# Moving a pair of reductions, a row of gathers and two small products in a two-layer graph attention kernel

## The chip, the cores and the metric

The kernel runs on one core of one Trainium2 chip. The metric is the time of one execution on the device in microseconds (us); lower is better. A core has TensorE (PE, matrix products; PEld is its loading of weights), VectorE (DVE), ScalarE (ACT), GpSimd (POOL) and SyncE (SP, which here only issues transfers). Each works through its own queue of instructions in order, and semaphores order the engines among each other. Transfers between memory and the core's SBUF run on 16 DMA engines.

## The reference, cut to what matters

The input `x` holds 16 graphs of 1024 nodes with 256 features; `adj` is a 1024 x 1024 adjacency matrix that all graphs share. Layer 0 is a small network with two attention steps, of which the first sees all pairs of nodes (no mask) and the second only the edges of `adj`. Layer 1 is one more masked attention.

```python
def _gat(inp, adj_mask, W, a):                 # layer 0
    h = inp @ W
    f1, f2 = h @ a[:F_, 0], h @ a[F_:, 0]
    e = leaky_relu(f1[:, :, None] + f2[:, None, :], 0.2)
    if adj_mask is not None: e = where(adj_mask > 0, e, NEG_INF)
    return elu(softmax(e, axis=2) @ h)

def _L0_gnn_ref(x, adj, ...):
    out = relu(x @ mlp1_w + mlp1_b);  residual = out
    out = elu(_gat(relu(out), None, W_fc, a_fc)) + residual      # dense attention
    out = relu(out @ mlp2_w + mlp2_b);  residual = out
    return relu(elu(_gat(relu(out), adj, W_hand, a_hand)) + residual)

def _L1_gnn_ref(inp, adj, W, a):               # slope 0.01, masked
    ...
    return relu(softmax(e, axis=-1) @ h)

x = x + _L0_gnn_ref(maximum(layernorm(x), 0), ...)
x = x + _L1_gnn_ref(maximum(layernorm(x), 0), ...)
```

## The kernel before, in words

Everything is float32. A graph is called `b` (0 to 15). Its nodes lie on the 128 partitions in 8 tiles `t`, which form two halves `h` of four tiles. The names on the profile's lines are tiles of the program: `hm` a projection, `att` a block of attention weights (128 x 256), `o` an accumulated product. An `a` at the end stands for the masked attention of layer 0 (`Gnn0`), a `b` for that of layer 1 (`Gnn1`).

The dense attention (`Dense`) computes no 1024 x 1024 matrix. Because the leaky ReLU of `f1 + f2` has two straight pieces, each node needs a sum over the nodes with small `f2` and one over those with large `f2`. So the rows of `h` are scattered to memory in the order of `f2` (`scatter`, L525) and read back sorted (`xs`). In each partition running sums are made over the 8 rows that it holds (`sum_before`, L597 and L599, in `tt`; `sum_behind`, L610 and L612, in `xs`), and `write_table` (L604) writes them to memory as the **fine** table. Two matrix products with triangles of ones (`carry`, L621) make the sums over the partitions before and behind; ACT copies them (L624), and SP writes them to memory as the **coarse** table (L626). For each node, `count` (L554) gives its row in both tables. `gather` (L637) is an indirect transfer that POOL issues: first the fine row of each of 128 nodes comes to the tile `got`, then the coarse row is added to it in flight. There are eight fine and eight coarse ones for a graph, four for each half, of 128 rows x 1026 numbers (525 KB) each; a coarse gather waits for the fine one of its tile. `share` (L649 to L652) makes the four tiles' denominators from `got`, and its first instruction waits for four coarse gathers. `mean` combines both sums of a tile (ACT's `part`, L659; DVE's `hp`, L661). `merge` transposes `hp` on PE (`hpT`, L708) and goes on with the ELU on DVE and ACT (L710 to L718); POOL adds the result to `resT` (L719). The second MLP (`mlp2`, L726) follows.

A masked attention projects its 8 tiles (`project`, L322, with ACT's copy to `hm`, L324). Then `extremes` (L329 and L330) takes the largest and smallest `f2` of each partition, and `vectors` brings the maxima to all partitions with a transpose on PE (`extps`, L238) and derives the factors `qwd`. For each quarter `q` of the rows DVE makes eight blocks of weights (L373) and PE multiplies them (L384). `Gnn0.finish` (L396 to L400) normalizes a tile, `combine` has POOL make two sums (L408 and L409), and `update` adds the outcome to `x` on DVE (L413). `Gnn1.finish` and `update` are L420 to L426, and `store` (L429) has SP write half of the output.

The second layer norm takes the statistics of each tile (L262 and L263), an inverse root for each half on POOL (`root`, L267 and L268), centers (`hn`, L272) and transposes on PE (`nt`, L282, with ACT's L286).

The order is written out by hand. `at(lo, hi, steps)` gives each step a due time on a ruler of the author's; the steps are sorted by it, and PE, DVE, ACT and SP take their instructions in that order. Added dependencies keep POOL's in the same order. A step puts all its instructions at one place in each queue that it uses. Graphs overlap: in the stretch of graph `b`, PE does the masked attention of layer 0 of `b` (`oa`), parts of that of layer 1 of `b - 1` (`ob`), the projection for layer 1 of `b` (`pb`), while the dense attention of `b + 1` goes through sums, gathers and merges, and the first MLP and projection of `b + 2` (L451 and L465) fill in. The stretches of `b` = 1 to 13 have one pattern. The first graph and the last two have due times of their own in part.

These are the due times that the change touches or meets, from the start `base` of the stretch of `b` on the ruler:

```python
gathers(dense[b + 1], h, base + 44.5 + 3.5 * h, base + 55 + 7 * h)    # b >= 1
# Gnn0.combine, tiles 4 to 7: 40.4, 41.0, 47.4, 48.0;  root: 43.0 and 56.5
# carry 0 and 1: 38.9, 45.9;  the products oa of quarter 1 end about 32, of quarter 2 about 39
# extremes of Gnn1: 78.5;  share of half 0: 78.0;  mean: 78.2 to 79.7
```

In memory, the buffer of `got` for the first half is that of `tt`, and that for the second half is that of `xs`; so the fifth fine gather waits for `carry(1)`, which reads `xs`. The first fine gather waits for the four writes of the fine table.

Of the kernel before, what the change touches and what calls it, by code (L numbers as in the profile page):

```python
# [31 lines left out]
def fast_path(ctx: ExitStack, tc: tile.TileContext, alarm, x, adj, w1, b1, w2, b2, w_fc, a_fc,  # L32
# [27 lines left out]
    NH = N // HALF  # L60
    TH = HALF // P
# [20 lines left out]
    def load_x(b, name):  # L82
        xt = big.tile([P, NT, F], F32, tag="x", name=f"{name}_{b}", bufs=3)
        src = x[b].rearrange("(t p) f -> p t f", p=P)
        for part in ((slice(0, TH), slice(TH, NT)) if name == "xn" and b == 0 else (slice(0, NT),)):
# [17 lines left out]
                            base=0, channel_multiplier=-1)  # L103
# [118 lines left out]
    def at(lo, hi, steps):  # L222
        for i, step in enumerate(steps):
            table.append((lo + (hi - lo) * i / len(steps), len(table), step))
# [74 lines left out]
    def tiles(h):  # L299
        return range(h * TH, (h + 1) * TH)  # L300
# [450 lines left out]
    norm1, norm2, dense, gnn0, gnn1 = {}, {}, {}, {}, {}  # L751
# [16 lines left out]
    def each(f, *ranges):  # L768
        out = [()]
        for r in ranges:  # L770
            out = [o + (i,) for o in out for i in r]
        return [partial(f, *o) for o in out]
# [14 lines left out]
    def first_mlp(t0, b):  # L787
        steps = mlp_steps(b)
        at(t0 + 0.7, t0 + 8, steps[:HC])
        lo = t0 + (39.3 if b == 2 else 78.1)  # L790
        at(lo, lo + 7, steps[HC:])

    def dense_rows(t0, b):

        for t in range(NT):
            at(t0 + BETWEEN[t], t0 + BETWEEN[t], [partial(dense[b].project, t, 1)])

    def dense_begin(t0, b):
        d = dense[b]
        at(t0 - 38.5, t0 - 38.5, [d.columns])  # L800
        at(t0 - 36.8, t0 - 36.8, [d.send, partial(d.row, True)])
        at(t0 - 31.5, t0 - 31.5, [d.highest])
        at(t0 - 28, t0 - 12, each(d.rank, range(NT)))
        at(t0 - 33, t0 - 30.5, [partial(d.project, t, 0) for t in range(2)])
        at(t0 - 21, t0 - 8, [partial(d.project, t, 0) for t in range(2, NT)])
        scatters(d, t0 - 18.5, t0 - 4.5)
        at(t0 - 6, t0 - 6, [d.query])
        at(t0 - 4, t0 - 4, [d.read_sorted])
# [5 lines left out]
    def dense_sums(t0, b):  # L814
        d = dense[b]
        at(t0 - 3, t0 - 3, [d.sums_begin])
        for t, lo in enumerate((27, 25, 18.5, 16.3, 14.1, 12, 9.8, 8.2)):
            at(t0 - lo, t0 - lo, [partial(d.sign, t)])
        for h in range(2):
            at(t0 + 6.5 + 4 * h, t0 + 6.5 + 4 * h, [partial(d.sums_weights, h)])  # L820
            at(t0 + 7.5 + 5 * h, t0 + 12.5 + 5 * h, each(d.sum_before, tiles(h)))
        at(t0 + 13, t0 + 13, [partial(d.write_table, 0, 0)])
        at(t0 + 18, t0 + 18, [partial(d.write_table, 0, 1)])
        at(t0 + 18, t0 + 32, each(d.sum_behind, range(NT - 1, -1, -1)))
        at(t0 + 25, t0 + 25, [partial(d.write_table, 1, 1)])
        at(t0 + 32, t0 + 32, [partial(d.write_table, 1, 0)])
        at(t0 + 33, t0 + 33, [d.count])
        at(t0 + 38.9, t0 + 38.9, [partial(d.carry, 0)])
        at(t0 + 45.9, t0 + 45.9, [partial(d.carry, 1)])

    def gathers(d, h, lo, hi):
        at(lo, lo + 4, each(d.gather, [h], [0], range(TH)))
        at(hi, hi + 7, each(d.gather, [h], [1], range(TH)))

    def dense_end(t0, b):
        d = dense[b]
        late = 10 * last(b)
        for h in range(NH):
            lo = t0 + late + 78 + 13.4 * h
            at(lo, lo, [partial(d.share, h)])  # L840
            lo = t0 + late + 78.2 + 14 * h
            at(lo, lo + 1.5, each(d.mean, [h], range(TH)))
            merges(t0 + late + 85 + 13.2 * h, d, h)
        second_mlp(t0, b)
# [17 lines left out]
    def masked_first(t0, b):  # L862
        m, n = gnn0[b], norm2[b]
        at(t0 + 1, t0 + 1, [m.vectors])
        lo = t0 + 11
        if b in AHEAD:
            at(t0 + 3.4, t0 + 3.4, [m.send])
            at(t0 + 6, t0 + 6, [partial(m.row, True)])
            lo += 7
        else:  # L870
            at(t0 + 4, t0 + 4, [m.row])
        at(t0 + 4.5, lo - 1, each(m.scale, range(NT)))
        weights(m, 0, lo - 5.5, lo - 1)
        at(t0 + 10, t0 + 10, [partial(load_again, b)])
        at(t0 + 4.5, t0 + 11, each(dense[b].natural, range(NT // 2)))
        at(lo, lo + 28, each(m.product, range(NQ), range(NT)))
        for q in range(1, NQ):
            weights(m, q, lo - 5.5 + 7 * q, lo + 1 + 7 * q)
        for t in range(NT):
            end = lo + 7.2 + 7 * (t // 2) + 0.6 * (t % 2)  # L880
            at(end, end, [partial(m.finish, t)])
            at(end + 1.2, end + 1.2, [lambda t=t: m.combine(t, dense[b].o_nat)])
            at(end + 5.2, end + 5.2, [lambda t=t: m.update(t, xs[b])])
            end += 6.2 if last(b) or b == 0 else 9
            at(end, end, [partial(n.stats, t)])
        at(lo + 25, lo + 25, [partial(n.root, 0)])
        lo += 35.5 if last(b) or b == 0 else 38.5
        at(lo, lo, [partial(n.root, 1)])

    def last(b, n=1):  # L890
        return b >= NB - n

    def second_norm(t0, b):
        n, m = norm2[b], gnn1[b]
        if last(b):
            n.turn_at(t0 + 46.5, 0)
            n.turn_at(t0 + 49, 1, 1.6)
            lo = t0 + 50
        elif b == 0:
            n.turn_at(t0 + 47, 0)  # L900
            n.turn_at(t0 + 50.5, 1, 1.6)
            lo = t0 + 47.2
        else:
            n.turn_at(t0 + 60.3, 0, 7)
            n.turn_at(t0 + 67.3, 1)
            lo = t0 + 71
        at(lo, lo + 7, each(m.project, range(NT)))
        at(lo + 7.5, lo + 7.5, [m.extremes])
        if last(b, 2):
            at(lo + 7.8, lo + 7.8, [m.vectors])  # L910
            at(lo + 8.2, lo + 8.2, [m.row])
            at(lo + 8.3, lo + 9.5, each(m.scale, range(NT)))
        else:
            at(lo + 11, lo + 11, [m.vectors])
            at(lo + 24, lo + 24, [m.send])
            at(lo + 40, lo + 52, each(m.scale, range(NT)))
            at(base_of(b + 1) - 4.5, base_of(b + 1) - 4.5, [partial(m.row, True)])

    def masked_second(parts, b):

        m = gnn1[b]
        for q, lo in enumerate(parts):
            at(lo, lo + 7, each(m.product, [q], range(NT)))
            weights(m, q, lo - 5.5, lo - 0.1)
            for u in range(2):
                t = 2 * q + u
                end = lo + 7.2 + 0.6 * u
                at(end, end, [partial(m.finish, t)])
                at(end + 1.5, end + 1.5, [lambda t=t: m.update(t, xs[b])])
            if q % 2:  # L930
                end = lo + 10
                at(end, end, [lambda h=q // 2: m.store(h, xs[b], b)])
# [7 lines left out]
    def base_of(b):  # L940
        return b * PERIOD - SHORT * (b > 0)

    START = -168.0
    n, d = norm1[0], dense[0]
# [34 lines left out]
    for t in range(TH):  # L979
        lo = START + 95 + 7.1 * t  # L980
# [31 lines left out]
    for b in range(NB):  # L1012
        base, after_base = base_of(b), base_of(b + 1)
        masked_first(base, b)
        second_norm(base, b)
        if last(b):
            parts = [base + 65 + 7 * q for q in range(NQ)]
        elif last(b, 2):
            parts = [base + 86, base + 94.5, base + 107.5, after_base + 39]
        else:  # L1020
            parts = [after_base + lo for lo in (11, 46, 53, 60)]
        masked_second(parts, b)
        if b + 1 < NB:
            if b:
                dense_sums(base, b + 1)
            for h in range(NH):
                if b:
                    gathers(dense[b + 1], h, base + 44.5 + 3.5 * h, base + 55 + 7 * h)
                else:
                    gathers(dense[1], h, base + 16 + 12 * h, base + 22 + 25 * h)  # L1030
            dense_end(after_base - PERIOD, b + 1)
        if b + 2 < NB:
            first_mlp(base, b + 2)
            dense_rows(after_base - PERIOD, b + 2)
            dense_begin(after_base, b + 2)
        if b + 3 < NB:
            lo = after_base - PERIOD + 86
            at(lo, lo, [partial(load_first, b + 3)])
            first_norm(after_base, b + 3)
# [465 lines left out]
```

## Time and profile before

| | |
|---|---|
| median of 3 runs | 2363.75 us (2357.47 to 2365.26) |
| the profiled execution | 2357.62 us, of which the span of the trace is 2355.9 us |
| mean granted TensorE clock | 0.99 |
| fine gather L637, 124 of them | 1.04 us of POOL each (mean), 5.6 us from issue to landing (median) |
| coarse gather L637, 124 of them | 1.60 us of POOL each (mean), 10.5 us from issue to landing (median) |
| one stretch of the repeating part | about 140 us |

A line of instructions in order of time gives start and duration in us, engine, source line, operation, output and inputs, and in brackets the idle time of the engine before it and what ended that. A line of waits reads: engine, tile and line that waited; what it waited for; us in total, number of times, longest. In a table of stretches each engine's busy time stands with the number of its instructions; the last three columns are the granted clock, the busy share of the DMA engines and their GB/s.

### The profile page before, as it was taken

How to read it: one execution, taken by the hardware profiler on the slowest of the kernel's cores; microseconds unless marked ns; L12 is line 12 of the kernel's file. 1: busy time of each engine (PE TensorE's matmuls, PEld its weight loads, DVE VectorE, ACT ScalarE, POOL GpSimd, SP SyncE). 2: the span in 40 equal slices, each digit the busy share in tenths (PEclk: the TensorE clock that was granted, in tenths of full speed). 3: DMA queues.
4: the chain of work that ended last, by engine and by line, in shares of the span. 5: the costliest groups of instructions: out<-in, count | busy, mean ns of one | idle time of the engine just before them, and what ended most of it. 6: DMA issues, size and time to landing. Idle time of an engine off the chain costs nothing. (4 is left out here: it accounts for less than half of the span.)

```text
span 2355.9 us, 30815 instructions
## 1 busy us (share of the span) xinstructions
PE 2264.0 (96%) x9955; PEld 1750.0 (74%) x9955; DVE 1610.9 (68%) x4499; ACT 1243.7 (53%) x2740; POOL 954.7 (41%) x1216
## 2 busy tenths in 40 slices
PE   8989999999999999999999999999999999999897
PEld 6666777777868778787877868777786877778676
DVE  6666685766858577685866767586685857668554
ACT  5355645647365564745546374554736556473442
POOL 1153435264433536434263533535344352634320
PEclk9999999999999999999999999999999999999898
DMA  4558356572655746366573645657264564636500
GB/s 175 166 161 206 74 167 172 168 189 96 191 127 175 184 149 183 96 193 151 170 188 128 178 112 173 163 170 201 96 196 118 171 179 152 184 95 193 122 1 29
DMA packets 150762, 355.81 MB, mean 151 GB/s; under 512 B 11112, under 2 KB 62648, under 8 KB 146496
## 3 DMA queue, kind: packets, MB, share of 16 engines
q1 hardware_dynamic: 103968, 189.58, 26.4%
q0 software_dynamic: 45952, 163.99, 26.3%
q8 instruction: 82, 1.34, 0.2%
q14 instruction: 88, 0.72, 0.1%
q10 hardware_dynamic: 672, 0.17, 0.0%
HBM read 227.40 MB, written 126.30 MB: 150 GB/s over the span
## 5 line engine op out<-in xcount | busy, mean ns | idle before, releaser
L384 PE MATMUL ob<-hmb,attb 128*128 128x257 f32 x2048 | 466.7, 386 | 13.6 <-DVE attb L373 13.5
L465 PE MATMUL h<-wfc_sb,resT 128*128 128x257 f32 x2048 | 465.5, 380 | 0.0
L384 PE MATMUL oa<-hma,atta 128*128 128x258 f32 x2048 | 454.4, 382 | 3.1 <-DVE atta L373 2.9
L384 PEld LDWEIGHTS ob<-hmb,attb 128*128 128x128 f32 x2048 | 388.3, 192 | 79.1 <-ACT rb L422 12.5
L384 PEld LDWEIGHTS oa<-hma,atta 128*128 128x128 f32 x2048 | 387.1, 190 | 65.1 <-DVE atta L373 9.6
L465 PEld LDWEIGHTS h<-wfc_sb,resT 128*128 128x128 f32 x2048 | 379.4, 190 | 53.5 <-issue 0.7
L719 POOL TENSOR_TENSOR resT<-resT,e 128x512 f32<-128x512 f32 x128 | 163.3, 1276 | 386.9 <-DVE e L718 343.4
L408 POOL TENSOR_TENSOR posa<-posa,onat 128x256 f32<-128x256 f32 x120 | 100.8, 840 | 468.2 <-ACT posa L400 467.6
L373 DVE SCALAR_TENSOR_TENSOR atta<-rowsa,qwda,edge 128x256 f32<-128x256 f32 x512 | 268.2, 554 | 24.0 <-PE oa L384 12.6
L373 DVE SCALAR_TENSOR_TENSOR attb<-rowsb,qwdb,edge 128x256 f32<-128x256 f32 x512 | 237.2, 505 | 9.9 <-PE ob L384 7.4
L451 PE MATMUL m<-hT,w_sb 128*128 128x512 f32 x512 | 236.2, 599 | 0.5 <-ACT posa L400 0.5
L726 PE MATMUL m<-resT,w_sb 128*128 128x512 f32 x512 | 231.5, 599 | 4.4 <-POOL resT L719 4.4
L422 ACT ACTIVATE rb<-ob,recb 128x256 f32<-128x256 f32 x128 | 59.1, 475 | 332.1 <-DVE recb L420 320.4
L637 POOL DMA_INDIRECT got<-coarse,k x124 | 198.1, 1598 | 39.0 <-issue 35.4
L399 ACT ACTIVATE ea<-oa,reca 128x256 f32<-128x256 f32 x128 | 60.8, 475 | 267.6 <-DVE reca L396 267.6
L710 DVE TENSOR_SCALAR e<-hpT 128x512 f32<-128x512 f32 x128 | 88.4, 690 | 141.3 <-PE hpT L708 108.8
L726 PEld LDWEIGHTS m<-resT,w_sb 128*128 128x128 f32 x512 | 94.1, 192 | 107.2 <-issue 91.3
L451 PEld LDWEIGHTS m<-hT,w_sb 128*128 128x128 f32 x512 | 93.0, 194 | 92.1 <-issue 89.7
L637 POOL DMA_INDIRECT got<-fine,k x124 | 128.9, 1040 | 55.4 <-DMA fine<-xs 23.9
L525 POOL DMA_INDIRECT sorted<-hnat,place x128 | 131.4, 1026 | 39.5 <-issue 20.3
L548 ACT ACTIVATE junk<-r,fs 128x1024 int8<-128x1024 f32 x124 | 142.4, 1149 | 5.7 <-POOL fs L469 4.7
L711 ACT ACTIVATE e<-e 128x512 f32<-128x512 f32 x128 | 80.7, 631 | 88.0 <-DVE e L710 87.9
(186 smaller groups left out, 3442.4 us busy)
## 6 DMA issues: line engine op xcount, KB each, us to landing
xs<-sorted SPq DMA_DIRECT2D x32, 1028.0 KB
fine<-tt SPq DMA_DIRECT2D x32, 1026.0 KB
fine<-xs SPq DMA_DIRECT2D x32, 1026.0 KB
x<-in_x_dram SPq DMA_DIRECT2D x16, 1024.0 KB
out_dram<-x SPq DMA_DIRECT2D x32, 512.0 KB
xn<-in_x_dram SPq DMA_DIRECT2D x15, 1024.0 KB
coarse<-carry SPq DMA_DIRECT2D x32, 256.5 KB
r<-row_r SPq DMA_DIRECT2D x14, 512.0 KB
```

The source lines that it names most:

```text
L373: nc.vector.scalar_tensor_tensor(a_t, self.rows[:, q * PAIR:(q + 1) * PAIR], self.qwd[:, 1, j:j + 1], edge[:, j, q * PAIR:(q + 1) * PAIR], ...
L384: nc.tensor.matmul(self.out[t][:, :F + self.ONES], lhsT=self.att[q, j][:, (t % 2) * P:(t % 2 + 1) * P], rhs=self.hm[:, j, 2:2 + F + self.O ...
L408: adder.tensor_add(pos, pos, o_nat[:, t, :])
L451: nc.tensor.matmul(ps, lhsT=w1_sb[:, kc, c * P:(c + 1) * P], rhs=hT[:, kc, h * HALF:(h + 1) * HALF], start=(kc == 0), stop=(kc == FC - 1))
L465: nc.tensor.matmul(ps[:, :F + 1], lhsT=self.resT[:, kc, t * P:(t + 1) * P], rhs=wfc_sb[:, kc, g, :], start=(kc == 0), stop=(kc == HC - 1))
L525: made = nc.gpsimd.indirect_dma_start(out=sorted_d[self.b % 2], out_offset=bass.IndirectOffsetOnAxis(ap=self.place[:, t:t + 1], axis=0), i ...
L548: nc.scalar.activation(junk, self.r2, AF.Sign, bias=self.fs[:, 0, t:t + 1], accum_out=self.signs[:, t:t + 1])
L637: nc.gpsimd.indirect_dma_start(out=got[u // n][:, u % n, :], out_offset=None, in_=(coarse_d if coarse else fine_d)[self.b % 2][:, :], in_o ...
L710: nc.vector.tensor_scalar_min(e, ps, 0.0)
L711: nc.scalar.activation(e, e, AF.Exp)
L719: nc.gpsimd.tensor_add(dst, dst, e)
L726: nc.tensor.matmul(ps, lhsT=w2_sb[:, kc, c * P:(c + 1) * P], rhs=self.resT[:, kc, h * HALF:(h + 1) * HALF], start=(kc == 0), stop=(kc == H ...
```

## The change

It does three things, all of them by other due times; no instruction is added or taken away.

1. `extremes` of the second layer's attention is due at `lo + 6.9` instead of `lo + 7.5`. In DVE's queue that puts L329 and L330 ahead of `share` of the first half; before, they stand behind `share` and the first `mean`. Nothing else changes its place on DVE.
2. From `b` = 1 on, `early_gathers` replaces `gathers`: the first four fine gathers are due at 41.5 and 42.5, the other four at 48.5 to 53, the coarse ones at 53.5 to 68. In POOL's queue, with S4 to S7 for the sums of a tile, F and C for fine and coarse gathers of the first (0) and second (1) half:

```
before, b = 1 to 3 and 8 to 14:  S4 S5 root0 F0 F0 F0 S6 F0 S7 F1 F1 F1 F1 C0 root1 C0 C0 C0 C1 C1 C1 C1
before, b = 4 to 7:              S4 S5 root0 F0 F0 F0 S6 F0 F1 S7 F1 F1 F1 C0 root1 C0 C0 C0 C1 C1 C1 C1
after:                           S4 S5 F0 F0 F0 F0 root0 S6 S7 F1 F1 F1 F1 C0 C0 root1 C0 C0 C1 C1 C1 C1
```

3. Both carries are due 7 earlier. On PE `carry(0)` moves from between the quarters 2 and 3 of `oa` to between 1 and 2, and `carry(1)` from behind quarter 3 to ahead of it. ACT's copies move with them, ahead of `finish` of tile 2 and of tile 4. On SP the write of the first carry moves ahead of the last write of the fine table.

```diff
-        at(t0 + 38.9, t0 + 38.9, [partial(d.carry, 0)])
-        at(t0 + 45.9, t0 + 45.9, [partial(d.carry, 1)])
+        at(t0 + 31.9, t0 + 31.9, [partial(d.carry, 0)])
+        at(t0 + 38.9, t0 + 38.9, [partial(d.carry, 1)])
...
+    def early_gathers(d, t0):
+
+        fine, coarse = [each(d.gather, range(NH), [s], range(TH)) for s in range(2)]
+        at(t0 + 41.5, t0 + 41.5, fine[:2])
+        at(t0 + 42.5, t0 + 42.5, fine[2:4])
+        at(t0 + 48.5, t0 + 53, fine[4:])
+        at(t0 + 53.5, t0 + 68, coarse)
...
-        at(lo + 7.5, lo + 7.5, [m.extremes])
+        at(lo + 6.9, lo + 6.9, [m.extremes])
...
-            for h in range(NH):
-                if b:
-                    gathers(dense[b + 1], h, base + 44.5 + 3.5 * h, base + 55 + 7 * h)
-                else:
+            if b:
+                early_gathers(dense[b + 1], base)
+            else:
+                for h in range(NH):
                     gathers(dense[1], h, base + 16 + 12 * h, base + 22 + 25 * h)
```

## The prediction

> **What bounds the kernel now.** I read the shares of busy time first, then the waits of TensorE, then one repeating stretch in order of time. TensorE (PE) is busy for 96% of the span, so at most some 92 us of idle time can be won; the table of PE's waits says where it lies.
>
> ```profile
> PE 2264.0 (96%) x9955; PEld 1750.0 (74%) x9955; DVE 1610.9 (68%) x4499; ACT 1243.7 (53%) x2740; POOL 954.7 (41%) x1216
> ...
> PE extpsb L238 <- DVE extb L330: 22.0, 13, 2.7
> PE nt L282 <- DVE hn L272: 15.4, 8, 9.7
> PE ob L384 <- DVE attb L373: 13.5, 20, 2.1
> PE hpT L708 <- DVE hp L661: 6.4, 7, 1.7
> ```
>
> The largest wait is for the two extremes of `extb` (L329, L330), which are tiny instructions. In order of time, 11 of the 13 stretches from `b` = 1 to 13 have it, 0.9 to 2.7 us each, 20.5 us together (two more of 0.76 us are in the last two elements and wait for another thing). Those of `hn` and `hpT` lie almost wholly at the beginning and the end. The order of time for `b` = 13 shows what the extremes stand behind (start, duration, engine; in brackets the idle time before and who ended it):
>
> ```profile
> 2048.09 1.55 POOL L637 DMA_INDIRECT got<-coarse,k  x1 [0.30 <-issue]
> ...
> 2058.43 0.16 DVE L649 TENSOR_TENSOR den<-got,qd 128x4 f32<-128x4 f32 x1 [9.60 <-DMA got<-coarse,k]
> ...
> 2059.99 0.75 DVE L661 SCALAR_TENSOR_TENSOR hp<-got,den,part 128x513 f32<-128x513 f32 x1 [0.79 <-ACT part L659]
> 2060.66 0.16 DVE L329 TENSOR_REDUCE extb<-hmb 128x1 f32<-128x8 f32 x1
> 2060.74 0.16 DVE L330 TENSOR_REDUCE extb<-hmb 128x1 f32<-128x8 f32 x1
> 2060.81 2.29 DVE L661 SCALAR_TENSOR_TENSOR hp<-got,den,part 128x513 f32<-128x513 f32 x3
> ```
>
> ```profile
> 2060.97 0.29 PE L238 MATMUL extpsb<-ident,extb 128*128 128x128 f32 x1 [1.84 <-DVE extb L330]
> 2061.10 1.88 PE L451 MATMUL m<-hT,w_sb 128*128 128x512 f32 x4
> 2062.82 0.67 PE L708 MATMUL hpT<-ident,hp 128*128 128x128 f32 x4
> ```
>
> The fourth coarse gather is issued at 2048.09 and lands after 10.2 us. The vector engine (DVE) sits idle for 9.60 us until then. In all 13 stretches PE starts L238 2.53 to 2.55 us after that landing, so PE is tied to the landing; and the next thing PE needs, `hpT`, comes only 1.85 us later and depends on the same landing.
>
> **What the skill says.** The Trainium skill, "DMA: Bandwidth & Descriptors", section "Issuing engines are not separate DMA queues", says that transfers of all issuing engines interleave on the same 16 DMA engines. The trace agrees, and shows where they are full (PE, PEld, DVE, ACT, POOL busy; then clock, DMA share, GB/s):
>
> ```profile
> 2035.00:2039.00 4.00, 3.93 (x20) 3.10 (x19) 3.70 (x12) 0.95 (x2) 3.24 (x4) 1.00 0.63 210
> 2039.00:2043.00 4.00, 4.00 (x24) 3.37 (x22) 3.66 (x13) 0.22 (x1) 3.31 (x5) 1.00 0.83 287
> 2043.00:2067.00 24.00, 22.16 (x95) 16.09 (x94) 9.71 (x30) 14.08 (x31) 12.15 (x9) 1.00 1.06 236
> ```
>
> "SBUF — State Buffer", section "Who interferes with whom", says that a DVE instruction with two SBUF inputs contends with a GpSimd instruction that reads SBUF. It agrees: L413 takes 0.41 us alone and 0.94 us beside GpSimd's (POOL's) sums. "PSUM — Partial Sum Buffer", section "Engine vs sequencer instructions", says that these engines' queues are strictly first in, first out; every start in these rows agrees.
>
> **Part 1, the extremes.** Nothing is added. They move ahead of `share` of the first half, to 2054.4, when the last `hmb` copy ends and DVE is idle: cost nothing, hidden in the 9.60 us. The 1.84 us wait goes. What is late next is `hpT`. PE would pass L238 at 2059.13 (2060.97 less 1.84), do 0.11 + 1.72 us of work to 2060.96, and then need four `hp` tiles. They end at 2063.10 now; with the two extremes (0.15 us together in issue) gone from between them, the second could end 0.15 us sooner, but the last two wait for ACT's `part` tiles, two buffers in turn at some 0.75 us each, which start when the first `hp` ends, at 2060.7, as now. I take 0.07 us (bounds 0 and 0.15). So 1.84 us of wait at L238 becomes some 1.8 us at L708: over 13 stretches the gain is 13 x 0.07 = 0.9 us, not 20.5.
>
> **Part 2, the gathers.** Only a sooner landing helps further. These rows are POOL's queue now:
>
> ```profile
> 2025.92 1.12 POOL L268 TENSOR_TENSOR rstd<-rstd,power 128x4 f32<-128x4 f32 x1
> 2027.24 1.12 POOL L637 DMA_INDIRECT got<-fine,k  x1 [0.20 <-issue]
> ...
> 2032.57 1.14 POOL L637 DMA_INDIRECT got<-fine,k  x1
> ...
> 2035.41 1.14 POOL L637 DMA_INDIRECT got<-fine,k  x1
> ...
> 2040.79 1.65 POOL L637 DMA_INDIRECT got<-coarse,k  x1 [0.30 <-issue]
> ```
>
> In the changed order all four fine gathers of the first half follow the sums of tile 5 in one row, then come `root(0)`, the sums of tiles 6 and 7, the other four, two coarse, `root(1)`, six coarse. They are not two and two between sums. From 2021.37 POOL has one gap, 0.90 us, before the sum of tile 4, and nothing is moved into it. So the first fine gathers start at 2025.6 instead of 2027.24, the fourth at 2029.5 instead of 2032.57; but the 5.2 us of four gathers, 1.6 us of `root(0)` and 2 x 1.5 us of sums end at 2035.3 in either order. The fifth gather stays at 2035.4, the first coarse at 2040.8, the fourth at 2048.1. Could the DMA engines still finish sooner? The fifth fine gather lands 5.4 us after its issue, as the very first does, so the earlier ones do not hold it up now. From 2043 the engines are full. What is unused between 2038.5 and 2043 is about 0.8 us (shares of 0.6 to 1.1 in half-microsecond slices), and only a sooner fifth gather could use it. The second coarse gather comes 1.3 us sooner, into full engines. I take 0 here (bound: 0.8 us gained).
>
> The loss: the sum of tile 6 ends at 2033.7 instead of 2032.4, so L413 and a weight (L373) that now run with POOL on gathers run beside the sum of tile 7. L413 goes from 0.42 to 0.94 us, L373 from 0.48 to 0.9; POOL's two adds go from 0.73 and 0.72 to 0.91 and 0.79. That puts the fifth gather about 0.2 us later, which the unused 0.8 us after it can take up: I take 0 at the landing (bound: 0.4 us lost a stretch). In four stretches (`b` = 4 to 7) two gathers stand ahead of the sum of tile 7 now, and PE loses 1.3 us there at L384 instead of 0.36; the change cures that, but PE waits for the landing afterwards all the same: nothing gained.
>
> `root(1)` moves behind the second coarse gather: it ends at 2045.9 instead of 2043.86. `hn` of the second half starts then instead of at 2044.96; queued behind it on DVE are two reciprocals, two updates and the second store of `out`, all about 1 us later. PE's transposes at 2045.96 wait for `hn`, a new wait of 0.7 us. It is hidden as long as PE has more than that before `hpT`, and it has about 1.8 us. In `b` = 14, with no such cover, I count 0.7 us. `root(0)` comes at 2032 and is needed at 2036.1: nothing.
>
> **Part 3, the carries.** Each is four passes, 0.87 us of PE, moved past 7 us of `oa` products; PE's total stays. The sums they read are done (`all_t` at 1997.7, the last `xs` at 2011.3; they would run at 2008 and 2015.9). ACT's copies go ahead of tiles 2 and 4, which wait for DVE until 2013.36 and 2020.45: nothing. SP's write of the first carry goes past the last fine write, ready about 2010 against 2011.3: nothing. PE reaches `oa`'s later products 0.87 us later, so seven waits for `atta` of 0.4 us may go; they too lie ahead of the landing.
>
> **The sum.** -0.9 + 0 + 0.7 = -0.2 us; with the bounds, -(0.15 + 0.8) x 13 = -12 and 0.4 x 13 + 0.7 = +6 us. On the profiled execution's own time, 2357.62 us (a span of 2355.9 and 1.7 around it), this is 2357.4. The median of the runs is 2363.75, 6 us above that execution, within the 8 us over which the runs spread; on it the sum gives 2363.5 us, no change. Within 0.3%, 7 us, is about what a measurement of this kernel cannot tell from nothing.
>
> **Rivals.** (a) The landing does move. If the early gathers and the second coarse one free the DMA engines, all the 0.8 us is won: 13 x 0.9 = 12 us, 2352 us; if the landing is 1.8 us sooner, the whole 20 us, 2344 us. For it: PE is tied to the landing in every stretch, so each 0.1 us there is 1.3 us. Against it: the fifth gather's unobstructed 5.4 us and a POOL queue without holes. The second half caps it: its `hp` are ready at 2076.8, just before PE's 2076.99. (b) Slower: POOL's sums of tiles 6 and 7, now back to back beside DVE's updates, hold back the fifth gather and with it both landings. At 0.4 us and with no part of it absorbed it is 5 us; it decides (over 7 us) from 0.55 us a stretch, and 0.8 us gives 13 x 0.8 = 10 us, 2374 us. For it: POOL is the link ahead of the DMA, with no slack. Against it: two DVE instructions only collide. (c) The change does not begin the gathers that matter sooner; that is my forecast.
>
> **How the numbers follow.** The forecast has 0.53, rival (a) 0.30, rival (b) 0.17. The range 2344 to 2373 takes in the whole of (a) and most of (b); the likeliest case alone is 2357 to 2370.
>
> **What would show it.** Right: PE's wait for `extb` falls from 22 us to some 2, and a wait of `hpT` for `hp` (L661) of 15 to 25 us stands in its place; the first coarse gather starts about 19.4 us after the sum of tile 4; `nt` waits some 0.7 us for `hn` in each stretch. Wrong: DVE's wait for the coarse landing ends more than 0.5 us sooner or later, counted from the sum of tile 4, or waits for `hp` stay under 8 us.

## The result, and the profile after

| | median, us | runs | lowest to highest |
|---|---|---|---|
| before | 2363.61 | 20 | 2354.8 to 2371.03 |
| after | 2356.84 | 20 | 2350.22 to 2361.55 |

The ratio is 0.9972, with a 95% interval of 0.9963 to 0.9980: 6.8 us, 0.28%, less. That lies within the 0.3% that the prediction called no change and inside its range, just below the 2357 to 2370 us of its likeliest case, but it is a gain all the same, and 6.6 us more than the sum of -0.2 us. The profiled execution took 2353.15 us with a span of 2351.4 us (before: 2357.62 and 2355.9).

The busy times of the page after:

```profile
PE 2271.9 (97%) x9955; PEld 1751.2 (74%) x9955; DVE 1620.2 (69%) x4499; ACT 1241.4 (53%) x2740; POOL 955.0 (41%) x1216
```

PE's busy time rose by 7.9 us though it does the same work. The groups of `nt` and `hpT` are 5.5 and 3.8 us longer, most likely because short waits inside a group count as busy, so a part of the waiting has only changed its name. The rest is in the table of PE's waits after (us in total, times, longest):

```profile
PE nt L282 <- DVE hn L272: 21.4, 23, 9.7
PE hpT L708 <- DVE hp L661: 11.8, 23, 1.7
PE ob L384 <- DVE attb L373: 11.6, 17, 2.1
...
PE extpsb L238 <- DVE extb L330: 1.5, 2, 0.8
```

The wait for `extb` went from 22.0 to 1.5 us, `hpT` from 6.4 to 11.8, and `nt` has 15 short waits more. The stretch of `b` = 13 after, in order of time, DVE first:

```profile
2050.96 0.17 DVE L329 TENSOR_REDUCE extb<-hmb 128x1 f32<-128x8 f32 x1 [5.48 <-ACT hmb L324]
...
2053.27 0.17 DVE L649 TENSOR_TENSOR den<-got,qd 128x4 f32<-128x4 f32 x1 [2.07 <-DMA got<-coarse,k]
```

The extremes stand alone ahead of the landing, and DVE waits twice, first for `hmb` and then for the landing. PE in the same stretch:

```profile
2042.11 1.43 PE L282 MATMUL nt<-ident,hn 128*128 128x128 f32 x8 [0.43 <-DVE hn L272]
...
2055.50 0.27 PE L238 MATMUL extpsb<-ident,extb 128*128 128x128 f32 x1
...
2057.33 0.85 PE L708 MATMUL hpT<-ident,hp 128*128 128x128 f32 x4
...
2059.76 0.60 PE L708 MATMUL hpT<-ident,hp 128*128 128x128 f32 x4
```

L238 has no wait left. The second group of `hpT` starts 6.48 to 6.50 us after the landing in all 13 stretches; before it was 6.63, in `b` = 13 here (the landing is at 2058.43):

```profile
2065.06 0.60 PE L708 MATMUL hpT<-ident,hp 128*128 128x128 f32 x4
```

So PE is still tied to the landing, one instruction further on. POOL, the sum of tile 4 before and then after:

```profile
2021.37 0.73 POOL L408 TENSOR_TENSOR posa<-posa,onat 128x256 f32<-128x256 f32 x1 [2.83 <-ACT posa L400]
```

```profile
2017.24 0.72 POOL L408 TENSOR_TENSOR posa<-posa,onat 128x256 f32<-128x256 f32 x1 [2.83 <-ACT posa L400]
...
2028.53 0.72 POOL L409 TENSOR_TENSOR ea<-ea,posa 128x256 f32<-128x256 f32 x1
2029.21 0.73 POOL L408 TENSOR_TENSOR posa<-posa,onat 128x256 f32<-128x256 f32 x1
2030.02 0.79 POOL L409 TENSOR_TENSOR ea<-ea,posa 128x256 f32<-128x256 f32 x1
2030.97 1.08 POOL L637 DMA_INDIRECT got<-fine,k  x1 [0.17 <-issue]
```

The fifth fine gather (2030.97) comes 13.7 us after the sum of tile 4; before it was 14.0. The first coarse one comes at 19.1 instead of 19.4.

Where the 4.5 us of span went: the first landing (`b` = 1) comes 1.9 us sooner, the twelve periods from there to the landing of `b` = 13 take 1673.52 instead of 1676.74 us, and the end takes 0.7 us more.

The landing is the number to follow. In every kernel below I took the start of L649 of the first half less the start of the sum of tile 4, and the same for the second half, each as a mean over the 13 stretches of the one profiled execution. Three kernels that leave the gathers where they were give 37.19, 37.37 and 37.39, so differences of 0.2 us are noise. The lost clock is the sum of 1 less the granted clock over a table of stretches of 1 us; what it means comes with the kernel one later.

| kernel | first half, us | second half, us | lost clock, 250 to 2150 us | ratio to before, 95% interval |
|---|---|---|---|---|
| before | 37.19 | 49.11 | 1.7 | 1 |
| after | 36.89 | 48.89 | 1.7 | 0.9972 (0.9963 to 0.9980) |
| extremes alone | 37.37 | 49.31 | 5.1 | 1.0001 (0.9990 to 1.0012) |
| gathers alone | 36.64 | 48.49 | 0 | 0.9961 (0.9946 to 0.9976) |
| carries alone | 37.39 | 49.34 | 3.4 | 1.0006 (0.9996 to 1.0017) |
| fine gathers early alone | 36.79 | 48.78 | 6.8 | 0.9978 (0.9966 to 0.9990) |
| second coarse gather ahead of root(1) alone | 37.01 | 48.95 | 1.7 | 0.9985 (0.9975 to 0.9995) |
| fourth coarse gather one later | 39.65 | 51.68 | 23.9 | 1.0194 (1.0167 to 1.0220) |
| first half first | 32.96 | 49.17 | 10.2 | 1.0006 (0.9992 to 1.0019) |
| in turn | 35.40 | 49.01 | 0 | 0.9962 (0.9948 to 0.9976) |
| after, stores late | 36.26 | 46.99 | 1.7 | 0.9953 (0.9938 to 0.9968) |
| before, stores late | 36.52 | 47.34 | 1.7 | 0.9940 (0.9916 to 0.9963) |
| in turn, stores late | 35.03 | 46.48 | 1.5 | 0.9904 (0.9877 to 0.9932) |
| the same without parts 1 and 3 | 34.51 | 45.86 | 1.7 | 0.9865 (0.9848 to 0.9881) |

The same starts divide each period in two: from the sum of tile 4 to the landing, and from the landing to the next sum of tile 4. The second part is 102.5 to 102.7 us on average in eleven of these kernels, before and after among them. So in these eleven, what an edit wins or loses in a stretch shows ahead of the landing. The three others are one later (103.8), in turn (103.7) and first half first (107.5), where PE pays behind the landing, as shown below.

### The profile page after: what moved, and what is told of

Same layout as the page of the kernel before. It is cut to its first block, busy times and chain, and to the rows that moved or that the text cites. A ratio compares the mean times of both kernels' runs of the same rounds, so it can differ in the third digit from the quotient of the medians.

```text
span 2351.4 us, 30828 instructions
## 1 busy us (share of the span) xinstructions
PE 2271.9 (97%) x9955; PEld 1751.2 (74%) x9955; DVE 1620.2 (69%) x4499; ACT 1241.4 (53%) x2740; POOL 955.0 (41%) x1216
## 5 line engine op out<-in xcount | busy, mean ns | idle before, releaser
L384 PE MATMUL ob<-hmb,attb 128*128 128x257 f32 x2048 | 467.7, 386 | 11.8 <-DVE attb L373 11.6
L465 PEld LDWEIGHTS h<-wfc_sb,resT 128*128 128x128 f32 x2048 | 379.5, 190 | 53.5 <-issue 0.7
L373 DVE SCALAR_TENSOR_TENSOR attb<-rowsb,qwdb,edge 128x256 f32<-128x256 f32 x512 | 243.6, 518 | 11.0 <-PE ob L384 8.4
```

Source lines behind the costliest of these rows:

```text
L373: nc.vector.scalar_tensor_tensor(a_t, self.rows[:, q * PAIR:(q + 1) * PAIR], self.qwd[:, 1, j:j + 1], edge[:, j, q * PAIR:(q + 1) * PAIR], ...
L384: nc.tensor.matmul(self.out[t][:, :F + self.ONES], lhsT=self.att[q, j][:, (t % 2) * P:(t % 2 + 1) * P], rhs=self.hm[:, j, 2:2 + F + self.O ...
L465: nc.tensor.matmul(ps[:, :F + 1], lhsT=self.resT[:, kc, t * P:(t + 1) * P], rhs=wfc_sb[:, kc, g, :], start=(kc == 0), stop=(kc == HC - 1))
```

## The experiments

### One part at a time

**Extremes alone.**

```diff
-        at(lo + 7.5, lo + 7.5, [m.extremes])
+        at(lo + 6.9, lo + 6.9, [m.extremes])
```

> The kernel before with part 1 alone: extremes due at lo + 6.9, gathers and carries as before. My theory (PE is tied to the landing of the fourth coarse gather, and the extremes only decide which wait stands there): the wait of extpsb for extb falls from 22.0 us to about 2, a wait of hpT for hp of some 1.5 us a stretch takes its place, the landing counted from the sum of tile 4 stays within 0.2 us of 37.2, and the time falls by 0.07 to 0.15 us a stretch, 1 to 2 us (ratio about 0.9995). Rival: the extremes are the whole change, and this kernel shows all of its 6.7 us (ratio 0.997).

Measured: 2361.60 us (14 runs), ratio 1.0001. PE's waits of this kernel:

```profile
PE hpT L708 <- DVE hp L661: 21.9, 43, 1.7
...
PE extpsb L238 <- DVE extb L330: 1.5, 2, 0.8
```

20.5 us of waiting left `extb` and 15.5 us came back at `hpT`. Together with 7 us that PE's group of `hpT` is longer "busy" (85.3 instead of 78.2) that makes up for all of it. The second `hpT` group starts at 6.49 us after the landing instead of 6.63, so the gain is 0.14 us a stretch, 1.8 us, too little to be seen in the time. The rival is out.

**Carries alone.**

```diff
-        at(t0 + 38.9, t0 + 38.9, [partial(d.carry, 0)])
-        at(t0 + 45.9, t0 + 45.9, [partial(d.carry, 1)])
+        at(t0 + 31.9, t0 + 31.9, [partial(d.carry, 0)])
+        at(t0 + 38.9, t0 + 38.9, [partial(d.carry, 1)])
```

> The kernel before with part 3 alone: both carries due 7 earlier. My theory: the landing stays at 37.2 us after the sum of tile 4 and the time within 1 us of before (ratio 0.9995 to 1.0005), with the waits of oa for atta down from 2.9 us to about 1.2. Rival: the carries are what brings the landing forward (the fifth gather stands behind carry(1) and the coarse ones behind its write): landing at 36.9 and 3 us or more off the time.

Measured: 2361.42 us (22 runs), ratio 1.0006, landing unmoved. The eight waits of `oa` for `atta` (2.9 us) are gone from the table, and those of `ob` for `attb` went from 13.5 to 15.9 us: PE arrives sooner at products whose weights DVE makes no sooner. The rival is out.

**Gathers alone**: `early_gathers`, with extremes and carries as before.

> The kernel before with part 2 alone: early_gathers, extremes and carries as before. My theory: the landing comes some 0.3 us sooner after the sum of tile 4 (36.9 instead of 37.2), PE still waits for extb, about 20 us in all, and the time falls by 2 to 4 us (ratio 0.998 to 0.999). Rival: the gathers alone move nothing, because the fifth waits for carry(1), which is made sooner only in part 3: ratio within 0.0005 of 1, landing 37.2.

Measured: 2350.78 us (9 runs), ratio 0.9961. PE's waits:

```profile
PE extpsb L238 <- DVE extb L330: 11.5, 15, 1.6
...
PE ob L384 <- DVE attb L373: 5.5, 3, 2.1
```

All that the change brings is in this part, and the two others add nothing to it: the interval of the whole change overlaps with this one. The wait for `extb` stands where it stood, only shorter. The waits for `attb` fell too, by 8.0 us, but those of the stretches lie 14 to 18 us behind the sum of tile 4, ahead of a landing that PE waits for anyway: with the fine gathers early alone they fall by the same 8.0 us, and the wait for `extb` grows by 4.2. The rival is out: the fifth gather comes sooner although `carry(1)` does not.

### Which half of the gathers

**Fine gathers early, root(1) still behind the first coarse gather.**

```diff
-        at(t0 + 53.5, t0 + 68, coarse)
+        at(t0 + 55, t0 + 62, coarse[:4])
+        at(t0 + 62, t0 + 69, coarse[4:])
```

(against the kernel with the gathers alone)

> The kernel before with half of part 2: the four first fine gathers in one row behind the sum of tile 5, root(1) still behind the first coarse gather. Theory A (POOL loses less where sums and gathers don't alternate): the fifth gather starts 13.7 us after the sum of tile 4 instead of 14.1, and most of the 0.55 us by which the landing came sooner with both halves of part 2 is here: landing at 36.8, ratio 0.996 to 0.998. Theory B (the second coarse gather ahead of root(1) fills the DMA engines): landing at 37.1, ratio 0.9995. In both, PE's transposes nt do not wait for hn in each stretch (15 us in all as before, not 21).

**Second coarse gather ahead of root(1), fine gathers as before.**

```diff
-        at(hi, hi + 7, each(d.gather, [h], [1], range(TH)))
+        coarse = each(d.gather, [h], [1], range(TH))
+        if d.b >= 2 and h == 0:
+            at(hi, hi + 2, coarse[:2])
+            at(hi + 3.5, hi + 7, coarse[2:])
+        else:
+            at(hi, hi + 7, coarse)
```

(against before)

> The kernel before with the other half of part 2: root(1) behind the second coarse gather instead of the first, fine gathers as before. Theory A: the landing stays at 37.0 to 37.2 us after the sum of tile 4, PE waits 21 us for hn instead of 15, ratio within 0.001 of 1. Theory B: the landing comes some 0.5 us sooner (36.7) and the ratio is 0.996 to 0.998.

Measured: 2356.48 us (22 runs, 0.9978) and 2357.25 us (22 runs, 0.9985). Both halves bring something, 0.22% and 0.15%, and their sum, 0.37%, is that of the gathers alone, 0.39%. Neither theory holds alone. The fifth gather is 13.7 us behind the sum of tile 4 in the first and stays at 14.0 in the second, as expected. PE's waits for `hn` are 15.4 us in the first and 19.8 in the second. The landings (36.79 and 37.01) point the same way, but the second is within the noise.

### Is the landing what sets the time?

**The fourth and fifth coarse gather exchanged**, in the kernel after.

```diff
+        coarse[3], coarse[4] = coarse[4], coarse[3]
         at(t0 + 53.5, t0 + 68, coarse)
```

> The kernel after with the fourth and fifth coarse gather exchanged, so that the first half's last one is issued 1.9 us later. Theory (the landing of the first half sets PE's time): it lands 2.5 to 3 us later, about 39.6 us after the sum of tile 4, the waits of PE for hp grow by that in each of 13 stretches, and spells of half clock of 1.71 us follow in many of them: 33 to 55 us slower than after, ratio to before 1.011 to 1.021. Rival (PE has slack behind the landing since the extremes are out of the way): within 5 us of after, ratio below 1.

Measured: 2407.60 us (5 runs), ratio 1.0194, and PE's waits:

```profile
PE hpT L708 <- DVE hp L661: 44.6, 58, 2.8
```

The first half lands 2.76 us later than after. Times 13 that is 36 us, yet the time is 50.8 us longer. The rest shows in the granted clock. Here are four stretches of the kernel before (us; PE, PEld, DVE, ACT, POOL busy; then clock, DMA share, GB/s), two at the wait of `b` = 12 and two at that of `b` = 10:

```profile
1916.33:1919.74 3.41, 1.34 (x4) 0.27 (x2) 1.28 (x5) 1.34 (x2) 0.00 (x0) 1.00 1.06 224
1919.74:1923.15 3.41, 3.04 (x5) 1.51 (x6) 3.13 (x11) 3.01 (x7) 0.00 (x0) 0.50 1.07 225
...
1636.43:1639.85 3.42, 1.77 (x5) 0.46 (x3) 0.67 (x4) 0.66 (x2) 0.00 (x0) 1.00 1.08 228
1639.85:1643.26 3.41, 2.34 (x9) 1.28 (x10) 3.25 (x7) 3.12 (x6) 0.00 (x0) 1.00 1.07 224
```

In `b` = 12 the clock is at half for 3.4 us after PE's wait of 2.4 us, which costs 1.71 us on top; the first `hpT` of that stretch starts 5.89 us behind the landing instead of 4.39. The Trainium skill, "TensorE: Matmul & The Clock Gate", section "What's actually happening", says that a window of about 3.4 us, which runs freely, decides between half and full clock. The traces agree: between 250 and 2150 us every spell lasts 3.41 us or twice that, and in each of the 14 profiles the spells begin whole multiples of 3.413 us apart (in before at 168.70, 1919.74 and 2192.80 us, which is 513 and 80 of them). But the page speaks of an idle window, and here a partly idle one was enough. Of the windows that ran at full clock in these profiles, all 96 in which PE was idle for 2.05 us or more were followed by half clock, 58 of the 141 with 1.3 to 2.05 us, and none of some 9000 with less. The other waits for `extb` in before drew none: the longest, 2.7 us in `b` = 10, is cut by the end of a window into 1.65 and 1.07 us, while 2.07 us of the wait in `b` = 12 lie in one. What decides between 1.3 and 2.05 us stays open.

In the kernel one later, 12 of these events lose 23.9 us between 250 and 2150 us; after has 1.7. From the landing of `b` = 1 to that of `b` = 13 it takes 48.7 us more than after, 33.0 of them ahead of the landings and 15.7 behind them, where the spells lie. So both are paid, the 22 us of lost clock not in full. In `b` = 3 of that kernel one sees what it does to PE:

```profile
677.15 3.64 PE L465 MATMUL h<-wfc_sb,resT 128*128 128x257 f32 x8
...
681.44 1.93 PE L465 MATMUL h<-wfc_sb,resT 128*128 128x257 f32 x8
```

The same eight products take 3.64 us at half clock and 1.93 when it is full.

### Orders that land sooner

**First half first**: behind the sum of tile 7 all four coarse gathers of the first half.

```diff
-        at(t0 + 48.5, t0 + 53, fine[4:])
-        at(t0 + 53.5, t0 + 68, coarse)
+        at(t0 + 48.5, t0 + 52, coarse[:4])
+        at(t0 + 57, t0 + 60, fine[4:])
+        at(t0 + 61, t0 + 68, coarse[4:])
```

> The kernel after with another order of the gathers: the four coarse ones of the first half straight behind the sum of tile 7, then root(1), then the four fine and the four coarse ones of the second half. The same number of transfers. My theory (the landing of the first half sets PE's time): the fourth coarse gather is issued some 21 us after the sum of tile 4 instead of 26.5, lands at about 31 instead of 36.9, PE's waits for hp of the first half (about 1 to 1.8 us a stretch) vanish, and 13 to 26 us go (ratio 0.989 to 0.9945), if the second half lands no later than now, 48.7 after that sum; I expect 46. Rival 1: the DMA engines are the limit, the second half lands later than 49, and PE waits there instead: slower by up to 10 us. Rival 2: PE is not tied to the landing any more, and the time stays within 2 us of after (ratio 0.997).

Measured: 2363.51 us (14 runs), ratio 1.0006. The expected gain is not there. The fourth coarse gather is issued at 19.7 us instead of 26.5, and DVE finds the first half landed when it comes to it at 32.96; PE waits for nothing there. But the first coarse gather of the second half is held until about 31 us, for the fine one that is now issued at 23, the second half lands at 49.17, and the wait is at its `hpT`, 25.2 us in 52 waits over the program. Six spells of half clock come with them, 10.2 us in all. This is rival 1 with its loss: the ratio is 0.34% above that of after, some 8 us, and the intervals do not meet.

**In turn**: coarse and fine alternate behind the sum of tile 7, `root(1)` in their middle.

```diff
-        at(t0 + 48.5, t0 + 53, fine[4:])
-        at(t0 + 53.5, t0 + 68, coarse)
+        both = [step for pair in zip(coarse[:4], fine[4:]) for step in pair]
+        at(t0 + 48.5, t0 + 54, both[:4])
+        at(t0 + 57, t0 + 60, both[4:])
+        at(t0 + 61, t0 + 68, coarse[4:])
```

> The kernel after with another order of the gathers behind the sum of tile 7: first coarse, fifth fine, second coarse, sixth fine, root(1), third coarse, seventh fine, fourth coarse, eighth fine, then the other four coarse. My theory (PE waits for the landings, and a PE wait of over some 1.4 us within 3.4 us also costs a spell of 3.4 us at half its clock, 1.71 us, as the traces so far show): the first half lands at or before 34 us after the sum of tile 4 instead of 36.9 and the second before 48.7, so that PE's waits for hp (12 us) and for hn of the second half (0.3 us a stretch in the record) go, with no spell of half clock from 250 to 2150 us; 10 to 20 us below after, ratio to before 0.989 to 0.993. Rival: as in the kernel with the first half first, the second half lands later (49 us or more), PE waits there, and several such spells follow: ratio 0.998 to 1.002.

Measured: 2353.46 us (13 runs), ratio 0.9962, which cannot be told from after. The first half lands 1.5 us sooner, the second at 49.01 as in the rival, and PE waits 14.7 us for `hp` between 300 and 2120 us. None of these waits draws a spell of half clock; the kernel with the first half first, whose spells lose 10.2 us, is 10 us slower.

### The transfers beside the gathers

**Stores late**, in the kernel after:

```diff
-                end = lo + 10
+                end = lo + 10 if last(b, 2) else base_of(b + 1) + 107.6 + 0.05 * q
                 at(end, end, [lambda h=q // 2: m.store(h, xs[b], b)])
```

> The kernel after with both stores of a graph (512 KB each, L429) issued some 50 us later, behind the broadcast of row_r, when the DMA engines are idle; SP then also issues the 1 MB load of xn sooner, ahead of the gathers instead of behind the stores. No other order changes. Theory (both landings are set by DMA engines that are full from 22 to 46 us after the sum of tile 4, and two of the 5.7 MB there are not gathers): the first half lands at 33 to 35 us after that sum instead of 36.9, the second before 46 instead of 48.7, PE's waits for hp in the stretches (some 7 us in the record, and as much hidden in groups) go, and no spell of half clock is left from 250 to 2150 us: 8 to 20 us below after, ratio to before 0.989 to 0.994. Rival (the coarse gathers are limited by their own descriptors, not by what runs beside them): landings within 0.5 us of after, ratio 0.997.

Measured: 2354.01 us (11 runs), ratio 0.9953, which cannot be told from after. The second half lands 1.9 us sooner, the first only 0.6. Two stretches of 12 us from 22 us behind the sum of tile 4 on, of after:

```profile
2039.24:2051.24 12.00, 11.57 (x55) 9.15 (x54) 3.17 (x12) 5.61 (x15) 10.39 (x8) 1.00 1.04 232
2051.24:2063.24 12.00, 11.96 (x48) 7.48 (x47) 7.09 (x19) 8.86 (x17) 2.95 (x3) 1.00 1.07 223
```

and the same two with the stores late:

```profile
2036.45:2048.45 12.00, 11.58 (x55) 9.16 (x54) 3.14 (x11) 5.57 (x15) 10.35 (x8) 1.00 1.00 194
2048.45:2060.45 12.00, 12.00 (x50) 7.82 (x49) 7.42 (x20) 9.11 (x18) 2.95 (x3) 1.00 0.91 178
```

A sixth to a fifth of the bytes is gone, and the DMA engines are as good as full without them. So the theory was half right: the stores delay the landings, but the coarse gathers fill the engines by themselves, and at fewer bytes than fine gathers alone in the same kernel:

```profile
2022.45:2026.45 4.00, 4.00 (x20) 3.49 (x20) 1.06 (x3) 0.90 (x3) 3.77 (x6) 1.00 0.95 368
```

PE waits no longer for `hp` here (0.8 us between 300 and 2120), but for `hn` (6.1) and `attb` (9.4).

**Stores late in the kernel before**, the same edit.

> The kernel before with the late stores alone: none of the three parts of the change. Theory (the landing is the cause, the order of the extremes only its display): the first half lands at 33.5 to 35.5 us instead of 37.2, the wait of extpsb for extb falls from 22 us to under 6, the one spell of half clock at 1919 us is absent, and the time falls by 15 to 25 us, ratio 0.989 to 0.994, more than the whole change brought. Rival: DMA traffic beside the gathers does not matter, extb stays at 20 us or more, ratio within 0.001 of 1.

Measured: 2351.19 us (6 runs), ratio 0.9940. The wait for `extb` falls to 14.8 us and the landing to 36.52, both less than expected, but the time is 12 us below the runs of before beside it (2363.39). It does at least as much as the whole change, without any part of it. Stores and load move together in this edit, so it does not show which of the two counts.

**In turn with stores late.**

> The late stores together with the gathers in turn (coarse and fine alternating behind the sum of tile 7). Theory: what held that order back was the second half's landing at 49 us; without the stores and the load it lands before 46, the first half's at 33, where DVE is the one that comes last, and PE waits neither for hp nor for hn: 10 to 25 us below after, ratio 0.987 to 0.993. Rival: as for the late stores alone, ratio 0.996 to 0.997.

Measured: 2340.62 us (6 runs), ratio 0.9904, faster than before and after. What each edit could not do alone (first half sooner, second half sooner), both do together; PE waits 0.2 us for `hp` and 0.8 for `hn` between 300 and 2120 us. Its waits for weights are another matter:

```profile
PE ob L384 <- DVE attb L373: 17.7, 19, 3.1
```

**The same with parts 1 and 3 undone**: extremes at 7.5, carries at 38.9 and 45.9.

> The fastest version so far (gathers in turn, late stores) with parts 1 and 3 of the change undone: extremes again behind the share and first mean of the first half, both carries at their old places. Theory (only the landings count): the landing stays at 35.0 us after the sum of tile 4; extpsb waits some 0.3 us a stretch for extb, since the extremes end 2.54 us after the landing and PE comes at 37.3; the time is 0 to 4 us above that version, ratio to before 0.989 to 0.993. Rival 1: with the landing no longer the bound, the extremes in front are worth their 1 to 2 us a stretch: 13 us or more above, ratio 0.996. Rival 2: this order needs the sooner carries, since the first coarse gather now starts 13.7 us after the sum of tile 4: coarse gathers start later, landing 36 or more, ratio 0.994 or more.

Measured: 2326.11 us (4 runs), ratio 0.9865: the fastest of all, 33.8 us below the runs of before beside it (2359.92). All three expectations are wrong in the sign: the version is not slower without the two parts, it is faster, or at the least no slower, since the intervals just touch (0.9877 and 0.9881). Its waits for weights:

```profile
PE ob L384 <- DVE attb L373: 6.7, 5, 2.4
```

They are 11 us shorter. A likely cause shows in the queues of SP and POOL, and it is in the profile of the kernel after as well. `b` = 10 of after, first SP, then POOL:

```profile
1586.23 0.33 SPq L626 DMA_DIRECT2D coarse<-carry  x1
1588.21 0.36 SPq L604 DMA_DIRECT2D fine<-xs  x1
...
1603.84 1.20 POOL L637 DMA_INDIRECT got<-fine,k  x1 [1.61 <-DMA fine<-xs]
```

With part 3 the write of the first carry (L626) goes to the DMA engines 2 us ahead of the last write of the fine table (L604), and the first fine gather, which part 2 has brought forward, waits for that write: 1.61 us here. In the kernel with the gathers alone the same gather starts 4.2 or 4.3 us behind the sum of tile 4 in all 13 stretches. After, it is 0.6, 1.5 and 1.0 us later than that in `b` = 6, 10 and 12, the two long ones waiting for this write; and the first halves of `b` = 10 and 12 land at 38.06 and 38.15. In the version in turn with late stores POOL waits five times, 9.3 us, for `fine<-xs`; with parts 1 and 3 undone, not once. There the first half lands at 36.0 us in the five stretches where the first fine gather is late by 0.8 us or more, and at 34.4 in the eight others, as without the two parts (34.5). The gathers that come late also hold the sums of tiles 6 and 7 behind them, and with them DVE's updates and weights, for which `ob` then waits.

Two things keep this from being settled. One later, first half first and in turn have parts 2 and 3 as well, and in their profiles this gather never waits for that write, so the delay does not come in every execution. And with the stores late, the write of the second carry is the last thing ahead of the load of `xn` on SP, so part 3 also starts that 1 MB load 7 us sooner (in `b` = 10 at 3.8 us ahead of the sum of tile 4 instead of 3.4 behind it), beside the end of the fine write. Parts 1 and 3 were undone together; that it is part 3 which costs is read from these waits and not shown by a run of its own.

## Why the prediction was right or wrong

**What bounds the kernel: right.** PE is tied to the landing of the first half's fourth coarse gather. One gather later is 51 us more. What the prediction did not have is the second price of a wait, 1.71 us of lost clock, which came from 1.3 us of idling in one window on.

**Part 1, extremes: right.** The 1.84 us at L238 went and came back at `hpT`. The term of 0.07 us a stretch was half of the truth, 0.14, the upper end of its bounds; alone it cannot be measured (1.0001). The sign "15 to 25 us at `hpT`" is met by the extremes alone (21.9) and missed by the whole change (11.8), because the landing moved and `nt` holds PE back first.

**Part 2, gathers: the step that failed is "I take 0 at the landing".** It has two terms. The first is POOL's time from the end of the fifth sum to the fifth fine gather: 9.95 us before (`b` = 13), for which the prediction counted the same and 0.2 us more for the collision; it is 9.63 (2030.97 less 2021.34). The collision is there: L413 takes 0.93 us beside the sum of tile 7 and the weight 0.94. But POOL's own add goes from 0.72 to 0.79 only. What the sum left out is that the same instructions take POOL less time in the new order: the first four gathers 3.92 us instead of 4.16, and `root(0)`, behind gathers instead of a sum, 1.38 instead of 1.61; the gaps and the collision give 0.15 of it back. Why they are shorter there no run shows. The second term is the second coarse gather, "into full engines": alone, moving it ahead of `root(1)` is worth 0.15% (0.9985). Together the landing is 0.30 us sooner after, and 0.55 us with the gathers alone, inside the bound of 0.8 us that rival (a) took whole. So rival (a) has the mechanism, and the forecast the size. That the total stayed within the 0.3% is in part luck: the gathers alone take 9 us off (0.39%), which is more than that, though the two intervals overlap.

**The new wait for `hn`: right.** It was to be 0.7 us a stretch, hidden, and 0.7 us in `b` = 14. In `b` = 13 it is 0.43 us ahead of a group that is itself 0.39 us longer, 1.43 instead of 1.04; in `b` = 14 it is 0.28 and 0.38. That it is hidden follows from the second coarse gather, which brings the wait and is faster all the same.

**Part 3, carries: right in its own kernel, wrong beside part 2 in the profile of after.** Alone it changes nothing (1.0006), and the `atta` waits went. The failed words are "SP's write of the first carry goes past the last fine write ...: nothing". The last fine write is issued no later, but the other write is on the DMA engines ahead of it, and part 2 takes away the 1.6 us of `root(0)` that would have covered it. Over the 13 stretches of this profile the first fine gather is some 3.4 us late in all. Three other kernels with both parts show no such wait, and the times of after and of the gathers alone cannot be told apart.

**Rivals.** (b), POOL's sums back to back, did not come about. The 6.8 us measured lie between the forecast and rival (a)'s 12. Of the signs, the fall of the `extb` wait and the short waits for `hn` came, but the first coarse gather comes at 19.1 us and not at 19.4; neither sign of being wrong appeared (the landing 0.30 us sooner, waits for `hp` 11.8 us).

## What to carry to other kernels

When a wait goes, ask at once which instruction needs the same event next: moving the two reductions only moved the wait, while each 0.1 us of the landing counted in all 13 stretches. A resource that two consumers share has to be freed for both of them: in the kernel after, landing the first half sooner, or moving the stores and the load away, brought nothing that could be measured alone, and together 16 us. A write that is moved ahead in a DMA queue can hold up the one behind it even if that is issued at the same moment, so look for who waits for the second one.

## What the runs showed of the hardware

- PE's clock was at half for 3.4 us (1.71 us lost) after windows of 3.413 us in which PE had idled for 2.05 us or more (96 of 96), after some with 1.3 to 2.05 us (58 of 141), and after none with less; eight products took 3.64 us instead of 1.93. A wait is therefore priced at its length plus a chance of 1.71 us, and where it falls among the windows matters: a wait of 2.7 us that a window's end divided was free of it. It also makes small differences in order look larger: the kernel with the first half first lost 10.2 us in this way.
- Coarse gathers, which add in flight, fill the DMA engines at fewer bytes: in the kernel after with the stores late they moved 178 GB/s at a busy share of 0.91, and fine gathers alone 368 GB/s at 0.95. Taking 38 to 45 GB/s of other transfers away moved the first landing by 0.6 us only.
